# Two transposes moved from TensorE to VectorE: Wv and the rows of sequences 3 and 4 loaded in blocks, with the rows of Wq, Wk and Wp in matching order

## The chip, the cores and the metric

The kernel runs on one core of one Trainium2 chip. The time is device microseconds of one execution; it was run three times. One further execution was taken by the hardware profiler, and all views of the profile come from that one. Engines are called PE (TensorE matmul), PEld (TensorE weight load), DVE (VectorE), ACT (ScalarE), POOL (GpSimd) and SP (SyncE, which only issues DMAs here). A line such as L489 is a line of the kernel before.

## The reference

Four sequences of 512 tokens with 512 features, all in fp32. An attention block, two feed-forward blocks and a low-rank adapter follow each other:

```python
q = x @ Wq; k = x @ Wk; v = x @ Wv                    # x [4,512,512], W* [512,512]
attn = softmax(q @ k.T * 512**-0.5)
attn_out = (attn @ v) @ Wp + bp
cms = gelu(attn_out @ cW1 + cb1) @ cW2 + cb2 + one_hot(codes)   # hidden 2048
mod = gelu(concat([attn_out, cms]) @ mW1 + mb1) @ mW2 + mb2
x1 = clip(x + cms + mod, 0, 1)
h = x1 + gelu(x1 @ W_down[stream] + b_down[stream]) @ W_up[stream] + b_up[stream]
out = (h - mean) * rsqrt(var + 1e-5) * ln_w[stream] + ln_b[stream]
```

## The kernel before, in words

The sequences are handled in two pairs. Features lie on partitions (four chunks of 128), tokens along the free dimension. All matmuls are fp32. Products are made by a scheme that needs seven block products in place of eight (on two levels in the feed-forward blocks); the price is sums of blocks, which DVE and POOL make.

**The folded weights.** The scores are x (Wq Wk^T) x^T, so the kernel first makes Wq Wk^T, and likewise Wv Wp (`folded`, L744). For a product both operands need the contracted index on partitions, so Wq, Wk, Wv and the rows of x are transposed first. PE does all of that: `begin_transposed` (L484) issues 16 transposes of 128x128 into four PSUM banks (`tr_ps`, L489), whose `end` then empties them; `turned_quarter` (L863, transposes at L868) does it for quarters of Wq and Wk.

**Where the transposed tiles go.** `left_from_psum` (L720, for Wv), `right_from_psum` (L677) and `second_operand.take` (L560, both for x) copy each bank to SBUF on ACT (L725, L683, L571) and make the block sums on DVE (L547, L558), part of them straight from PSUM.

**One product.** `seven` (L591) runs the seven block products in the order that it is given, in numbers 1 to 7, for one or two rows of blocks. Product 1 is copied out as c1 by ACT (L612); when product 5 is there, DVE adds c1 to it ("c15"); when 6 is there, DVE adds c15 to it into the bank of 5 ("the y sum"); when 7 has been accumulated onto 6, DVE makes v from it and c15 ("the v sum"), into a bank of its own; only then may product 4 accumulate further onto that bank. 3 accumulates onto y, 2 onto 1. `pair_product` (L632, matmuls at L637) uses the order 1, 2, 5, 6, 7, 4, 3 on 512 columns for both sequences of a pair at once; `small_product` (L694, matmuls at L703) uses 256 columns. Work can be hung behind a number by `then`. The recording layer orders the instructions of each engine itself, by dependences and estimates, unless one is pinned by `keep_in_program_order`; so the order in the text is not quite the order on the engine. PSUM has eight banks, all from one pool.

**Order around the change.** SP loads Wq in quarters (ACT's queue Wk), then x of sequences 1 and 2 (`load_x`, L141), Wv and Wp (`weight`, L114), into big[0], big[1], slot[2], slot[3]. POOL's queue loads the first part of cW1 and x of 3 and 4 into slot[6], slot[7]. PE turns and multiplies Wq and Wk; x of 1 and 2 are turned in between (`first_operand`, `both_operands`, L839 and L845). The first `pair_product` (x times the folded matrix) has the transposes of Wv behind its product 7 (L932). Then Wv Wp, the scores and softmax of sequences 1 and 2 (L946, sums of the second's x by `left_sums` at L951), the products with the probabilities, and a second `pair_product` (L982), which has x of sequence 3 turned behind its product 6 and x of 4 behind its 4. The second pair follows in the same way without loads.

**POOL's background work.** `expansion` (L420) makes the block sums of cW1, cW2 and mW1 from 13 us to 339 us and stores them in DRAM through spaces that the pair's layers use later (`part`, `first`, `wide`); `steps` (L473) advances it. The layers load them by SP into `wslot`. From 207 us on SP's queue is in use; before that it is empty after the first loads. ACT's queue stores the turned x (`xT_kept`, L857), which POOL loads back and adds to cms much later (L1688, L1691).

Of the kernel before, what the change touches and what calls it, by code (L numbers as in the profile page):

```python
# [8 lines left out]
F32 = mybir.dt.float32  # L9
# [9 lines left out]
def kernel(  # L19
# [119 lines left out]
    make_identity(nc, ident)  # L139

    def load_x(b, eng, dst):  # L141
        eng.dma_start(out=dst, in_=x[b].rearrange("(t p) v -> p t v", p=P))
        return dst
# [51 lines left out]

    def weight_sums(a11, a12, a21, a22, s1, s2, s3, s4, eng=None):
        eng = eng or nc.gpsimd
        eng.tensor_tensor(s1, a21, a22, ALU.add)
        eng.tensor_tensor(s2, s1, a11, ALU.subtract)
        eng.tensor_tensor(s3, a11, a21, ALU.subtract)  # L200
        eng.tensor_tensor(s4, a12, s2, ALU.subtract)  # L201

# [6 lines left out]


    def flat(t):
        return t.rearrange("p c n -> p (c n)")

# [229 lines left out]
    def inner_weights(src, is_first, store, p, u):  # L443
# [27 lines left out]
        }  # L471

    def steps(gen, n):  # L473
        for _ in range(n):
            next(gen, None)

# [7 lines left out]
    def begin_transposed(get, dst, finish=None):  # L484

        ps = [bank("tr_ps") for d in range(4)]
        for c in range(4):
            for d in range(4):
                nc.tensor.transpose(  # L489
                    ps[d][:, c * P : (c + 1) * P], get(c)[:, d * P : (d + 1) * P], ident  # L490
                )

        def end():
            for d in range(4):
                if finish is None:
                    evacuate(dst[:, d, :], ps[d])
                else:
                    finish(d, ps[d])

        return end  # L500

    def chunks(t):
        return lambda c: t[:, c, :]

# [162 lines left out]

    def left_sums(t, s):
        weight_sums(*halves(t), *(s[:, k] for k in range(4)))

# [98 lines left out]

    xT_kept = [spill.tile([P, 4, 512], F32, name=f"xT_kept{b}") for b in range(B)]  # L770
    attn_kept = [spill.tile([P, 4, 512], F32, name=f"attn_kept{b}") for b in range(B)]
# [63 lines left out]
    def places(pair):  # L835

        return big[2 + 2 * pair : 4 + 2 * pair], (big[6:8], big[0:2])[pair]

    def first_operand(pair):  # L839
        xT, t_x = places(pair)  # L840
        return begin_transposed(
            chunks(x_rows[2 * pair]), xT[0], right_from_psum(xT[0], sums_in(flat(t_x[0])))
        )

    def both_operands(pair):  # L845
        xT, _ = places(pair)
        operands, take = second_operand(*xT, mod)
        beside = right_from_psum(xT[1], sums_in(flat(places(pair)[1][1])), copy=False)
        transposed(
            chunks(x_rows[2 * pair + 1]), xT[1],  # L850
            lambda d, ps: take(
                d // 2, (slice(d % 2, d % 2 + 1), slice(0, 512)),
                ps.rearrange("p (c n) -> p c n", c=1), lambda: beside(d, ps),
            ),
        )
# [56 lines left out]
    for pair in range(B // 2):  # L912
# [14 lines left out]
        if pair == 0:  # L927
# [14 lines left out]
        def turn(k):  # L942
            transposed(lambda t: mod[k][:, t, :], pT[k], right_from_psum(pT[k], t_p[k]))

        for k in range(2):
# [711 lines left out]
    for pair in range(B // 2):  # L1657
# [144 lines left out]
```

## Time and profile before

| | us |
|---|---|
| three runs | 1171.57, 1169.13, 1168.83 |
| median | 1169.13 |
| profiled execution, its own time | 1169.93 |
| profiled execution, span from the first to the last instruction | 1168.2 |
| PE busy | 1158.7 (99%) |
| DVE busy | 893.8 (77%) |
| POOL busy | 588.6 (50%) |
| ACT busy | 293.2 (25%) |

In the table of busy times a matmul's record includes its way through the array, and records overlap. So a group's own cost on PE is read from the start of one group to the start of the next in the chain of waits, not from the mean length of a record. A record of an fp32 matmul appears twice (two passes), that of a transpose once. For DVE and ACT too, the step from one instruction to the next in a run without idle time is shorter than a record: 0.60 us against 0.69 for 128x512 on DVE.

The phases by start time: folding of Wq and Wk to 25 us, first pair's attention to 129, its projection with the turning of x of 3 and 4 to 143, second pair's attention to 243, the first pair's feed-forward blocks to 676, the second pair's to the end, with the first pair's adapters inside.

### The profile page before, as it was taken

How to read it: one execution, taken by the hardware profiler on the slowest of the kernel's cores; microseconds unless marked ns; L12 is line 12 of the kernel's file. 1: busy time of each engine (PE TensorE's matmuls, PEld its weight loads, DVE VectorE, ACT ScalarE, POOL GpSimd, SP SyncE). 2: the span in 40 equal slices, each digit the busy share in tenths (PEclk: the TensorE clock that was granted, in tenths of full speed). 3: DMA queues.
4: the chain of work that ended last, by engine and by line, in shares of the span. 5: the costliest groups of instructions: out<-in, count | busy, mean ns of one | idle time of the engine just before them, and what ended most of it. 6: DMA issues, size and time to landing. Idle time of an engine off the chain costs nothing.

```text
span 1168.2 us, 13723 instructions
## 1 busy us (share of the span) xinstructions
PE 1158.7 (99%) x4989; PEld 927.4 (79%) x4989; DVE 893.8 (77%) x1215; ACT 293.2 (25%) x535; POOL 588.6 (50%) x652
## 2 busy tenths in 40 slices
PE   9999999999999999999999999999999999999997
PEld 8588558657468888888888887778888888888875
DVE  5755655587699967899699956689994588689956
ACT  4244315236520000012310027271000003220014
POOL 4989999988897058982200636972000001242101
PEclk9999999999999999999999999999999999999999
DMA  9742784897766588896847662135745454594701
GB/s 336 268 139 100 297 323 176 307 382 253 300 240 245 185 282 313 322 328 263 258 157 279 191 215 90 64 143 179 299 132 188 168 216 180 176 307 165 246 6 73
DMA packets 81283, 256.80 MB, mean 220 GB/s; under 512 B 7956, under 2 KB 38976, under 8 KB 65984
## 3 DMA queue, kind: packets, MB, share of 16 engines
q1 hardware_dynamic: 56864, 152.98, 36.4%
q0 software_dynamic: 21968, 93.37, 22.7%
q10 hardware_dynamic: 2384, 9.57, 2.1%
q8 instruction: 40, 0.66, 0.2%
q14 instruction: 27, 0.22, 0.1%
HBM read 186.69 MB, written 66.06 MB: 216 GB/s over the span
## 4 chain that ended last, share of the span: by engine, by line
PE 94%; DVE 2%; POOL 1%; DMA 1%; issue 1%; DVEq 0%
PE i L1406 29%; PE i L1306 26%; PE sum L1148 9%; PE sum L703 9%; PE sum L637 8%; PE c L1238 6%; PE down_ps L1512 2%; PE up_ps L1531 2%; PE tr_ps L489 1%; DMA wslot<-in_L_cond_mW 1%; PE up_ps L1526 1%; DVE slot L206 1%; DVE hidden L547 1%; PE tr_ps L868 0%; PE idle_ps L193 0%
## 5 line engine op out<-in xcount | busy, mean ns | idle before, releaser
L1306 PE MATMUL i<-slot,wslot 128*128 128x256 f32 x1184 | 261.4, 379 | 1.3 <-DVE part L1010 1.2
L1306 PEld LDWEIGHTS i<-slot,wslot 128*128 128x128 f32 x1184 | 224.7, 190 | 32.8 <-issue 1.8
L1406 PE MATMUL i<-slot,wslot 128*128 128x256 f32 x896 | 202.5, 379 | 0.0
L1406 PEld LDWEIGHTS i<-slot,wslot 128*128 128x128 f32 x896 | 170.2, 190 | 23.1
L1017 ACT COPY first<-i 128x256 f32<-128x256 f32 (+1 forms) x56 | 26.7, 477 | 516.0 <-PE i L1406 255.6
L1406 PE MATMUL i<-hidden,wslot 128*128 128x256 f32 x576 | 132.2, 379 | 0.0
L1406 PEld LDWEIGHTS i<-hidden,wslot 128*128 128x128 f32 x576 | 109.4, 190 | 15.7 <-issue 1.0
L1010 DVE TENSOR_TENSOR part<-i,part 128x512 f32<-128x512 f32 (+1 forms) x156 | 90.5, 591 | 37.7 <-PE i L1306 25.4
L1039 ACT ACTIVATE hidden<-hidden,bias 128x512 f32<-128x512 f32 x128 | 83.9, 716 | 81.3 <-DVE hidden L547 71.3
L1688 POOL DMA_DIRECT2D slot<-xT_kept x4 | 2.7, 683 | 152.9 <-PE i L1306 152.9
L1148 PE MATMUL sum<-mod,wslot 128*128 128x256 f32 x288 | 66.7, 379 | 0.2 <-DVE sum L547 0.2
L206 DVE TENSOR_TENSOR slot<-hidden 128x1024 f32<-128x1024 f32 x46 | 61.3, 1332 | 0.0
L1148 PEld LDWEIGHTS sum<-mod,wslot 128*128 128x128 f32 x288 | 54.6, 190 | 7.9 <-DVE sum L547 0.6
L1691 POOL TENSOR_TENSOR cms<-cms,slot 128x512 f32<-128x512 f32 x16 | 24.4, 1548 | 71.3 <-PE i L1306 41.1
L1010 DVE TENSOR_TENSOR part<-i,first 128x512 f32<-128x512 f32 (+1 forms) x62 | 36.3, 589 | 29.0 <-PE i L1306 17.7
L547 DVE TENSOR_TENSOR sum<-sum,wslot 128x512 f32<-128x512 f32 x48 | 33.3, 696 | 31.5 <-PE sum L703 19.6
L206 DVE TENSOR_TENSOR slot<-hidden,slot 128x1024 f32<-128x1024 f32 x46 | 56.8, 1234 | 0.3
L1238 PE MATMUL c<-slot,wslot 128*128 128x512 f32 x128 | 55.3, 592 | 0.0
L547 DVE TENSOR_TENSOR hidden<-part,hidden 128x2048 f32<-128x2048 f32 x20 | 54.6, 2732 | 0.5
L703 PE MATMUL sum<-hidden,wslot 128*128 128x256 f32 x232 | 53.4, 380 | 0.6 <-POOL wslot L201 0.6
L703 PEld LDWEIGHTS sum<-hidden,wslot 128*128 128x128 f32 x232 | 43.7, 190 | 6.7 <-POOL wslot L201 1.0
L1238 PEld LDWEIGHTS c<-slot,wslot 128*128 128x128 f32 x128 | 24.3, 190 | 30.6 <-issue 27.5
(338 smaller groups left out, 2129.3 us busy)
## 6 DMA issues: line engine op xcount, KB each, us to landing
wslot<-m_kept SPq DMA_DIRECT2D x48, 1024.0 KB
wslot<-m_kept SPq DMA_DIRECT2D x36, 512.0 KB
wslot<-c_kept SPq DMA_DIRECT2D x16, 1024.0 KB
slot<-in_L_cond_mW POOLq DMA_DIRECT2D x24, 512.0 KB
wslot<-in_L_cond_mW SPq DMA_DIRECT2D x24, 512.0 KB
wslot<-in_L_cond_cW SPq DMA_DIRECT2D x40, 256.0 KB
slot<-in_L_cond_cW POOLq DMA_DIRECT2D x16, 512.0 KB
m_kept<-wide POOLq DMA_DIRECT2D x6, 1024.0 KB
```

Of the source, the lines that this page charges most:

```text
L206: i = eng.tensor_tensor(out_, one, two, ALU.subtract)
L547: nc.vector.tensor_tensor(dst, a, b, ALU.add)
L637: nc.tensor.matmul(ps, lhsT=lhs[p][:, c, r * P : (r + 1) * P], rhs=rhs[p][:, c, :], start=(first_ and c == 0), stop=(c == 1), skip_group_c ...
L703: nc.tensor.matmul(v[:, j, :], lhsT=lhs[p][:, c, j * P : (j + 1) * P], rhs=rhs[p][:, c, :], start=(first_ and j == 0 and c == 0), stop=(c ...
L1010: nc.vector.tensor_tensor(dst, ps, other, ALU.add)
L1017: nc.scalar.copy(c1, p1)
L1039: nc.scalar.activation(block[:, t, :], block[:, t, :], AF.Gelu, bias=bias_c[:, 8 * half + t : 8 * half + t + 1],)
L1148: nc.tensor.matmul(halves_of(ps)[:, j, :], lhsT=a[g][:, at_[q], j * P : (j + 1) * P], rhs=rhs[q][:, 0, :], start=(first_ and j == 0), stop ...
L1238: nc.tensor.matmul(ps, lhsT=lhs(c, t), rhs=operands[p][:, c, :], start=(c == 0), stop=(c == 1),)
L1306: nc.tensor.matmul(out_ps[:, j, :], lhsT=a[j][q][:, c, :], rhs=now[q][:, c, :], start=(c == 0), stop=(c == 1),)
L1406: nc.tensor.matmul(ps[:, :256], lhsT=a[k // 2][q][:, k % 2, :], rhs=now[q][:, k, :], start=(k == 0), stop=(k == 3),)
L1691: nc.gpsimd.tensor_tensor(cms[s][:, d, :], cms[s][:, d, :], in_rows[3][:, d, :], ALU.add)
```

## The change

Wv, and x of sequences 3 and 4, are loaded by four DMAs each, one for each group of 32 partitions: partition 32a + r receives, for each of the 16 groups t of 32 rows, the 128 consecutive elements (512 bytes) of row 32t + r that begin at column 128a. VectorE's transpose works on blocks of 32x32; four of its instructions, each of 128x512 with a step of four elements (16 bytes) on the input, turn the whole matrix into four PSUM banks, so that partition p of bank d holds column 4p + d. The 48 transposes of PE for these three matrices go.

The feature that partition p of chunk d stands for is thus 4p + d instead of 128d + p. Everything that is contracted with it follows: Wq, Wk and Wp are loaded with rows 4p + c (Wp by one DMA), and PE's transposes of x of sequences 1 and 2 read every fourth element. The turned x is stored to DRAM by features, and read back by 128c + p.

x of sequences 3 and 4 is needed untransposed as well, so SP loads it a second time into the same places once DVE has read them. The first load of these two moves in POOL's queue behind the first third of the expansion. The turning of Wv hangs behind product 6 of the first `pair_product` instead of 7. The sums of the x of sequence 2 are pinned, and the expansion's next steps are issued behind them.

```diff
@@ quarters (Wq, Wk)
-            rows, columns = slice(256 * r, 256 * r + 256), slice(256 * k, 256 * k + 256)
+            chunks, columns = slice(2 * r, 2 * r + 2), slice(256 * k, 256 * k + 256)
             eng.dma_start(
-                out=w[:, 2 * r : 2 * r + 2, columns],
-                in_=src[rows, columns].rearrange("(c p) n -> p c n", p=P),
+                out=w[:, chunks, columns],
+                in_=src.rearrange("(p c) n -> p c n", c=4)[:, chunks, columns],
             )
@@ loads
+    def load_blocks(src, dst, eng):
+        for a in range(4):
+            eng.dma_start(
+                out=dst[32 * a : 32 * a + 32].rearrange("p (t n) -> p t n", n=P),
+                in_=src[:, P * a : P * a + P].rearrange("(t r) n -> r t n", r=32),
+            )
+        return dst.rearrange("p (t c d) -> p d t c", d=4, c=32)
+
     x_rows = [load_x(b, nc.sync, x_places[b]) for b in range(2)]
-    wv = weight((nc.sync, nc.sync), Wv, slot[2])
-    wp = weight((nc.sync, nc.sync), Wp, slot[3])
+    x_blocks = []
+    wv = load_blocks(Wv, slot[2], nc.sync)
+    wp = slot[3].rearrange("p (c n) -> p c n", c=4)
+    nc.sync.dma_start(out=wp, in_=Wp.rearrange("(p c) n -> p c n", c=4))
@@ weight_sums
+        i = op(s1, a21, a22, ALU.add)
+        if pinned:
+            tc.keep_in_program_order(i)
...
@@ expansion
         load_c1(0)
+        yield from expand_c1(0, lambda: load_c1(1))
         for b in range(2, B):
-            x_rows.append(load_x(b, nc.gpsimd, x_places[b]))
-        yield from expand_c1(0, lambda: load_c1(1))
+            x_blocks.append(load_blocks(x[b], flat(x_places[b]), nc.gpsimd))
         yield from expand_c1(1, lambda: load_raw(cW2, False, 0, slot[4:6]))
@@ steps
+    behind = []
     def steps(gen, n):
-        for _ in range(n):
-            next(gen, None)
+        with tc.issue_after(behind.pop().ins) if behind else nullcontext():
+            for _ in range(n):
+                next(gen, None)
@@ transposes
+    def begin_turned(blocks, dst, finish=None):
+        ps = [bank("tr_ps") for d in range(4)]
+        for d in range(4):
+            nc.vector.transpose(ps[d].rearrange("p (t c) -> p t c", c=32), blocks[:, d])
+        def end():
+            for d in range(4):
+                if finish is None:
+                    evacuate(dst[:, d, :], ps[d])
+                else:
+                    finish(d, ps[d])
+        return end
+
+    def begin_x(b, dst, finish):
+        if b > 1:
+            return begin_turned(x_blocks[b - 2], dst, finish)
+        return begin_transposed(
+            lambda c: x_rows[b][:, c, :].rearrange("p (n d) -> p d n", d=4), dst, finish
+        )
@@ both_operands
         for k in range(2):
-            nc.scalar.dma_start(out=xT_kept[2 * pair + k], in_=xT[k])
+            nc.scalar.dma_start(
+                out=xT_kept[2 * pair + k].rearrange("(p c) n -> p c n", c=4), in_=xT[k]
+            )
+            if pair:
+                x_rows.append(load_x(2 + k, nc.sync, x_places[2 + k]))
@@ pairs
-            then[7] = [lambda: transposed(chunks(wv), wv_t, left_from_psum(wv_t, s_v))]
+            then[6] = [lambda: begin_turned(wv, wv_t, left_from_psum(wv_t, s_v))()]
...
-                left_sums(x_rows[s1], s_x[1])
+                behind.append(left_sums(x_rows[s1], s_x[1], pinned=True))
@@ with_input
-            tc.keep_in_program_order(nc.gpsimd.dma_start(out=in_rows[3], in_=xT_kept[2 * pair + s]))
+            tc.keep_in_program_order(nc.gpsimd.dma_start(out=in_rows[3], in_=xT_kept[2 * pair + s].rearrange("(c p) n -> p c n", p=P)))
```

More of the change, by code (lines that the diff above doesn't have):

```diff
@@ L1 @@
-from contextlib import ExitStack
+from contextlib import ExitStack, nullcontext
 import concourse.bass as bass
@@ L139, with flat @@
     make_identity(nc, ident)
+    def flat(t):
+        return t.rearrange("p c n -> p (c n)")
     def load_x(b, eng, dst):
@@ L193, with weight_sums @@
         nc.tensor.matmul(idle_ps[:, :P], lhsT=zeros, rhs=zeros, start=True, stop=True)
[L196 to L201, printed above, removed]
+    def weight_sums(a11, a12, a21, a22, s1, s2, s3, s4, eng=None, pinned=False):
+        op = (eng or nc.gpsimd).tensor_tensor
+        i = op(s1, a21, a22, ALU.add)
+        if pinned:
+            tc.keep_in_program_order(i)
+        op(s2, s1, a11, ALU.subtract)
+        op(s3, a11, a21, ALU.subtract)
+        return op(s4, a12, s2, ALU.subtract)
     def token_sums(b11, b12, b21, b22, t1, t2, t3, t4, eng=None, pinned=False):
@@ L208, in token_sums @@
                 tc.keep_in_program_order(i)
-    def flat(t):
-        return t.rearrange("p c n -> p (c n)")
     C1_PLAIN = {1: (0, 0), 2: (1, 0), 4: (1, 1)}
@@ L489, in begin_transposed @@
                 nc.tensor.transpose(
-                    ps[d][:, c * P : (c + 1) * P], get(c)[:, d * P : (d + 1) * P], ident
+                    ps[d][:, c * P : (c + 1) * P], get(c)[:, d], ident
                 )
@@ L500, in begin_transposed @@
         return end
+    def begin_turned(blocks, dst, finish=None):
[9 more added lines that the diff above has]
+        return end
     def chunks(t):
-        return lambda c: t[:, c, :]
+        return lambda c: t[:, c, :].rearrange("p (d n) -> p d n", n=P)
     def into(t):
@@ L666, in left_operand, with left_sums @@
         return {1: a11, 2: a12, 3: s4, 4: a22, 5: s1, 6: s2, 7: s3}
-    def left_sums(t, s):
-        weight_sums(*halves(t), *(s[:, k] for k in range(4)))
+    def left_sums(t, s, pinned=False):
+        return weight_sums(*halves(t), *(s[:, k] for k in range(4)), pinned=pinned)
     def right_operand(t, s):
@@ L768, in folded @@
         return left_operand(w, s)
-    xT_kept = [spill.tile([P, 4, 512], F32, name=f"xT_kept{b}") for b in range(B)]
+    xT_kept = [spill.tile([V, T], F32, name=f"xT_kept{b}") for b in range(B)]
     attn_kept = [spill.tile([P, 4, 512], F32, name=f"attn_kept{b}") for b in range(B)]
@@ L837, in places @@
         return big[2 + 2 * pair : 4 + 2 * pair], (big[6:8], big[0:2])[pair]
+    def begin_x(b, dst, finish):
[4 more added lines that the diff above has]
+        )
     def first_operand(pair):
         xT, t_x = places(pair)
-        return begin_transposed(
-            chunks(x_rows[2 * pair]), xT[0], right_from_psum(xT[0], sums_in(flat(t_x[0])))
+        return begin_x(
+            2 * pair, xT[0], right_from_psum(xT[0], sums_in(flat(t_x[0])))
         )
@@ L848, in both_operands @@
         beside = right_from_psum(xT[1], sums_in(flat(places(pair)[1][1])), copy=False)
-        transposed(
-            chunks(x_rows[2 * pair + 1]), xT[1],
+        begin_x(
+            2 * pair + 1, xT[1],
             lambda d, ps: take(
@@ L854, in both_operands @@
             ),
-        )
+        )()
         for k in range(2):
-            nc.scalar.dma_start(out=xT_kept[2 * pair + k], in_=xT[k])
+            nc.scalar.dma_start(
[3 more added lines that the diff above has]
+                x_rows.append(load_x(2 + k, nc.sync, x_places[2 + k]))
         return operands
@@ L942, in turn @@
         def turn(k):
-            transposed(lambda t: mod[k][:, t, :], pT[k], right_from_psum(pT[k], t_p[k]))
+            transposed(chunks(mod[k]), pT[k], right_from_psum(pT[k], t_p[k]))
         for k in range(2):
```

## The prediction

> **What bounds the kernel now.** I read the page's busy table first, then who waited for whom on PE, then the chain of waits in order of time, then the stages in which the removed work lies.
>
> ```profile
> PE 1158.7 (99%) x4989; PEld 927.4 (79%) x4989; DVE 893.8 (77%) x1215; ACT 293.2 (25%) x535; POOL 588.6 (50%) x652
> ```
>
> PE is busy for 1158.7 of 1168.2 us, so a microsecond taken from PE's queue is a microsecond of the span, unless a new wait replaces it. PE's waits before 220 us are two:
>
> ```profile
> PE idle_ps L193 <- DVE zeros L190: 1.1, 1, 1.1
> PE sum L703 <- POOL wslot L201: 0.6, 1, 0.6
> ```
>
> The chain, in order of time (start, length), passes through the transposes that the change takes away:
>
> ```profile
> 43.08 0.87 PE tr_ps L489 x8
> 43.95 1.72 PE sum L637 x4
> 45.67 0.44 PE tr_ps L489 x4
> ...
> 48.68 0.44 PE tr_ps L489 x4
> ...
> 111.89 3.72 PE sum L703 x16
> ...
> 129.35 1.75 PE tr_ps L489 x16
> ...
> 138.93 1.64 PE tr_ps L489 x15
> ```
>
> Wv is turned at 43 to 49 us, x of sequence 3 at 129 to 131, of sequence 4 at 135 to 141. Sixteen take 1.75 us, so one takes 0.109 us of PE however long its own record is (272 ns; records overlap). The two stages (length, then busy time and instructions of each engine):
>
> ```profile
> 25.00:51.00 26.00, 26.00 (x75) 12.43 (x74) 20.17 (x44) 9.23 (x18) 21.86 (x24) 1.00 0.76 277
> 129.00:150.00 21.00, 21.00 (x74) 11.15 (x73) 15.27 (x32) 9.10 (x16) 20.94 (x23) 1.00 0.71 285
> ```
>
> Third of the busy times is DVE: 20.2 of 26 and 15.3 of 21 us. DVE has room there, but not much, and it is DVE that gets the work.
>
> **The change part by part.** The sum is against the profiled execution: span 1168.2 us, time 1169.93, so 1.7 us lie around the span; it is 0.8 us above the median of the runs, 1169.13.
>
> *Removed from PE.* 48 of the 144 transposes of L489 (the group on slot tiles): 48 x 0.109 = 5.24 us, all on the chain. *Removed wait.* At 111.89 PE waited 0.58 us for POOL's sums of x of sequence 2 (L198 to L201 into wslot). In the new order these four stand right behind the second part of the cW1 expansion and ahead of the cW2 expansion. Adding POOL's rows up from 53.4 us (eight x loads, the five sums and six DMAs between) they end near 86, against a need at 109: 0.58 us gained.
>
> *Added on DVE.* Twelve block transposes of 128x512 elements, SBUF to PSUM, reading every fourth element (16 bytes apart). No such instruction and no such step is in the trace. The nearest rows:
>
> ```profile
> L547 DVE TENSOR_TENSOR sum<-sum,wslot 128x512 f32<-128x512 f32 x10 | 7.0, 697 | 7.8 <-PE sum L703 5.0 <-PE sum L637 2.9
> L198 POOL TENSOR_TENSOR wide<-slot 128x512 f32<-128x512 f32 x2 | 2.5, 1272 | 0.0
> 330.45 3.94 DVE L206 TENSOR_TENSOR slot<-hidden 128x1024 f32<-128x1024 f32 x1
> 344.62 1.23 DVE L206 TENSOR_TENSOR slot<-hidden,slot 128x1024 f32<-128x1024 f32 x1
> ```
>
> DVE's 128x512 operations record 0.69 us and follow each other every 0.60; ACT copies that size every 0.48, a floor; POOL works through it every 1.23 us; and one DVE operation from SBUF took 3.94 us beside busy POOL where its like takes 1.23, a factor of 3.2. So T, the step from one block transpose to the next, lies between 0.48 and about 1.9 us. I take 0.60, the row of the same engine, size and PSUM side, and walk both places in the built order.
>
> First place (before's clock). DVE ends the y sum of row 1 near 39.4 us, then does four transposes, eight 128x256 sums of Wv (0.33 each, 2.66), then the two v sums (0.60 each) that order 7 of the product leaves. PE ends order 7 at 42.06 and now does order 3 first (3.44 us) and one matmul of the next product (0.43), to 45.93; order 4 needs the first v sum, ready at 39.4 + 4T + 2.66 + 0.6 = 42.7 + 4T. At T = 0.60 that is 45.1: no stall; from T = 0.81 on PE waits; 1.6 us at 1.2; 4 at 1.8.
>
> Second place (clock from the product's start, 115.45). DVE: second c15 sum to 11.2, T, y, T, y, 2T, eight sums, v. The second y waits for PE until 13.9, so v is ready at 17.8 + 2T, or at 15.7 + 4T if that is later. PE needs it at 19.75. T = 0.60: 19.0, no stall. At 1.2: 0.8 us, and 0.4 more behind the second four, whose results the next product's orders 5 and 6 need. At 1.8 about 6 us, since both fours then hold up PE.
>
> So the wait costs 0 at 0.60, 2.9 at 1.2, about 10 at 1.8; a faster T than 0.60 gains nothing.
>
> [...]
>
> *Strided loads on PE.* The 32 transposes of sequences 1 and 2 stay, but load weights with a 16-byte step:
>
> ```profile
> L489 PEld LDWEIGHTS tr_ps<-ident,hidden x32: 139/140/143, 15.7 to 24.7; 128*128 128x128 f32 x32
> ```
>
> A load of 140 ns hides behind a step of 109. If the step lengthened it, PE could be held to at most the 190 ns of other fp32 loads: 32 x 0.081 = 2.6 us. A gain has no reason: the stream of columns is as long. I take 0.5, keep 0 and 2.6.
>
> *Costed at nothing.* Quarters of Wq and Wk: same 1 KB runs, same bytes. Wv in 512-byte runs: needed at 39 us instead of 43; at the 329 GB/s of the first 25 us the 6 MB up to it and Wp take some 19, so its own 1 MB (3 us) could take four times as long. POOL issues eight x loads in place of two: 8 x 0.76 against 1.51, +4.6 us on POOL near 55 us; 2.1 us of gathers move behind the expansion, and the 7.5 us wait of L361 for the c_outer store shrinks, so POOL reaches the cW2 sums some 2 us earlier. Reloading x of 3 and 4 on SP: its queue is empty until 207, the sums that read them are at 157 and about 170, issues at 129 and 138; behind them on SP stands only the attention reload of 207. The load of xT_kept in 2 KB runs on POOL: 0.1 us an issue, its sums have PE to wait for. If the POOL cover fails: at 336 to 350 DVE reuses wide, whose last store landed near 334.5 by its DMA packets, and PE then lives on its eight banks; 5 us of late POOL would cost 3 to 5 us.
>
> Sum: 1169.93 - 5.24 - 0.58 + 0.5 = 1164.6; for the median, 1169.13 - 5.3 = **1163.8**.
>
> **The rivals.**
> *B: block transposes at half pace (T = 1.2, as POOL's row).* 1169.13 - 5.8 + 2.9 + 0.5 = 1166.7; at T = 1.0 it is 1165. For it: the 16-byte step. Against: no row shows DVE slower for a layout.
> *C, slower: DVE becomes the bound in both places, because block transposes from SBUF stretch beside POOL as the row of 3.94 us did.* Price 10 us at T = 1.8: 1169.13 - 5.8 + 10 + 0.5 = 1173.8; it decides from T of about 1.45 on. For it: POOL is busy 20.9 of 21 us in the second place. Against: DVE's operations with one SBUF and one PSUM operand keep 0.60 there.
> *D: strided weight loads set PE's pace*, +2.6: 1165.9 with T = 0.60, more with B.
> *E: the gain is given back at 336 to 350 us*, where PE arrives 5 us earlier and POOL does not: about 1168.8. Against: 334.5 leaves 1.7 us to the 336.2 at which DVE would want wide, and POOL is some us earlier.
> That the change does not do what it says is excluded: the built PE queue has 48 transposes fewer.
>
> **How the numbers follow.** Forecast 0.45, B 0.27, C 0.20, D 0.05, E 0.03. A difference under 0.3% (3.5 us) is about what a measurement of this kernel cannot tell from none. Faster by more: the forecast and half of B (T up to 1.05), 0.45 + 0.13 = 0.58. Within: the rest of B 0.14, D 0.04, E 0.02 = 0.20. Slower: C 0.20, and 0.01 each of D and E = 0.22. The range goes from 1162.0 (all 5.8 us, no strided price, less the 1.3 us that a run may lie lower) to 1172.0, which takes in B, D, E and C up to T = 1.65, and leaves out about 0.1 of C and 0.05 below.
>
> **What would show it.** In the profile after: 96 transposes by PE at this line, steps of 0.109 us also for hidden tiles (D if their sixteens take over 2 us); twelve DVE transposes with a step of 0.60 (B near 1.2, C over 1.45); PE without a wait for DVE near 46 and 133 us, and none for POOL near 109; PE reaching the first c matmul (L1238) near 237.6 instead of 242.9 and the first L1306 as much earlier. The forecast is wrong if PE waits over 1 us for a v sum at either place, or if the lead at 243 us is there but gone at 420.

## Result, and the profile after

The changed kernel takes 1172.49 us (median of 22 runs, 1167.29 to 1178.41), the kernel before 1169.39 (22 runs, 1167.69 to 1171.57): a ratio of 1.0034, 95% interval 1.0023 to 1.0046. Predicted were 1163.8 us. It is slower by a third of a per cent, little, but the whole interval lies above 1, and its runs spread over 11.1 us instead of 3.9. Its profiled execution took 1172.08 us, span 1170.3, against 1169.93 and 1168.2 before.

In the profile after, L489 has become L506, the block transposes are L523, L547 is L579, L637 is L669, L703 is L735, L868 is L911, L1010 and L1017 are L1053 and L1060, L1238 is L1281, L1306 is L1349, L1326 is L1369, L1406 is L1449.

The busy table of the page, as shown of before:

```profile
PE 1155.4 (99%) x4941; PEld 923.0 (79%) x4941; DVE 904.5 (77%) x1227; ACT 294.1 (25%) x535; POOL 605.2 (52%) x658
```

PE has 48 instructions fewer and is busy for 3.3 us less, DVE has 12 more; yet the span is 2.1 us longer. Who waited for whom on PE (sum, times, longest):

```profile
PE i L1449 <- DVE cms L1053: 2.5, 1, 2.5
PE i L1449 <- ACT first L1060: 1.7, 1, 1.7
PE i L1349 <- DVE part L1053: 1.5, 1, 1.5
PE idle_ps L208 <- DVE zeros L205: 1.1, 1, 1.1
PE sum L669 <- DVE sum L579: 0.9, 1, 0.9
PE i L1349 <- DMA wslot<-in_L_cond_mW: 0.4, 2, 0.2
PE tr_ps L911 <- DMA wide<-in_L_cond_Wk: 0.2, 1, 0.2
```

The wait for POOL's sums is gone. Five rows are new: the two of L1449, which had no wait before, that of L669, and two short ones for loads. The chain that ended last shows what PE waited for; first the page's shares by engine, then pieces of the chain (start, length):

```profile
PE 72%; POOL 16%; DMA 6%; DVE 3%; issue 2%; ACTq 0%; DVEq 0%; POOLq 0%
```

```profile
2.30 8.49 DMA wide<-in_L_cond_Wk
...
40.51 4.11 DVE tr_ps L523 x4
48.11 3.70 PE sum L669 x8
51.81 32.81 PE sum L735 x152
...
204.59 8.56 DMA m_kept<-part
...
249.61 10.54 DMA m_kept<-part
...
336.59 4.16 DMA m_kept<-wide
```

Before, the chain was PE's for 94% and POOL's for 1%. Now it leaves PE at 86 us and follows POOL's expansion and the landing of its stores until 341 us. The two stages of the prediction (length, busy time and instructions of PE, PEld, DVE, ACT, POOL, granted clock, DMA share, GB/s):

```profile
25.00:51.00 26.00, 25.12 (x67) 11.63 (x66) 24.24 (x49) 8.97 (x17) 20.07 (x22) 1.00 0.62 225
129.00:150.00 21.00, 20.97 (x50) 9.11 (x49) 20.93 (x39) 9.10 (x15) 20.94 (x23) 1.00 0.87 299
```

DVE rises from 20.2 to 24.2 us of 26 and from 15.3 to 20.9 of 21: it is nearly full in the first place and full in the second.

**Where the time goes.** The start of the same PE work after, less its start before, through the run:

| at (time before) | after less before, us |
|---|---|
| 15.9, x of sequence 1 turned | +0.70 |
| 24.9, first pair product | +1.07 |
| 83.9, first softmax's transposes | +0.53 |
| 113.7, behind the removed POOL wait | -0.30 |
| 167.0 to 335.7, second pair, first c layer | -3.51 |
| 420.3, first L1349 | **+1.25** |
| 876.8 | +0.97 |
| 1046.0, and to the end | +1.84 |

So the change does bring 3.5 us (5.3 were expected), keeps them until 336 us, and loses 4.8 us in one layer. PE's order there, with its waits, and the ACT copy that it waits for:

```profile
344.32 1.89 PE L1449 MATMUL i<-hidden,wslot 128*128 128x256 f32 x8
347.93 1.99 PE L1449 MATMUL i<-slot,wslot 128*128 128x256 f32 x8 [1.72 <-ACT first L1060]
352.42 3.72 PE L1449 MATMUL i<-slot,wslot 128*128 128x256 f32 x16 [2.49 <-DVE cms L1053]
```

```profile
347.50 0.65 ACT L1060 COPY first<-i 128x256 f32<-128x256 f32 x2 [7.19 <-DMA m_kept<-first]
```

The copy goes into the space `first`, which POOL's expansion still uses: its last store from there has to land. POOL issues it at 342.94 us; before, at 338.32:

```profile
342.94 0.56 POOL L392 DMA_DIRECT2D m_kept<-first  x1
```

```profile
338.32 0.56 POOL L378 DMA_DIRECT2D m_kept<-first  x1
```

So PE is 3.5 us earlier and POOL 4.6 us later. The larger of the two waits, 2.49 us, comes another way, through DVE. DVE writes into `wide`, another of the expansion's spaces; its last store was issued at 336.59 us, 6.6 us later than before (329.95). DVE waits for its landing, and then its operation takes 4.09 us where it took 2.27 before (after, then before):

```profile
341.07 4.09 DVE L1369 TENSOR_TENSOR wide<-hidden,hidden 128x2048 f32<-128x2048 f32 x1 [1.55 <-DMA m_kept<-wide]
```

```profile
341.17 2.27 DVE L1326 TENSOR_TENSOR wide<-hidden,hidden 128x2048 f32<-128x2048 f32 x1
```

At this place of the run the operation took, in the fifteen profiles of this case, 2.27 or 2.28 us where POOL had issued its last store of the expansion before it began, and 3.5 to 4.3 us where POOL was not done. So a late POOL costs in two ways here: by the landing of its stores, and, as these profiles suggest, by slowing DVE.

**Why POOL is late.** Its first operation of the expansion, after and then before:

```profile
30.69 1.27 POOL L213 TENSOR_TENSOR wide<-slot 128x512 f32<-128x512 f32 x1 [9.50 <-DMA slot<-in_L_cond_cW]
```

```profile
29.09 0.72 POOL L198 TENSOR_TENSOR wide<-slot 128x256 f32<-128x256 f32 x1 [6.66 <-PE sum L637]
```

Before, cW1 is there and POOL waits for PE; after, POOL waits for cW1. While cW1 should arrive, the DMA engines are full and move half as much (stage 15 to 20 us, after and before; the last two columns are DMA share and GB/s):

```profile
15.00:20.00 5.00, 5.00 (x33) 4.62 (x32) 2.66 (x6) 1.68 (x4) 4.98 (x6) 1.00 1.22 181
```

```profile
15.00:20.00 5.00, 5.00 (x33) 4.55 (x32) 3.18 (x8) 2.05 (x4) 4.98 (x6) 1.00 1.05 388
```

What is loaded there is Wv, by groups of 32 partitions: SP issued its four DMAs from 6.95 to 13.93 us. The experiments take this up. By then the theories were: (1) POOL's expansion, late, sets the end, and PE's lead is lost to it, at first put down to the place of the sums of sequence 4; (2) POOL is late because of the more and smaller DMAs and the second load of x; (3) VectorE's block transposes are what costs.

### The profile page after: what moved, and what is told of

Same layout as the page of the kernel before. It is cut to its first block, busy times and chain, and to the rows that moved or that the text cites. A ratio compares the mean times of both kernels' runs of the same rounds, so it can differ in the third digit from the quotient of the medians.

```text
span 1170.3 us, 13661 instructions
## 1 busy us (share of the span) xinstructions
PE 1155.4 (99%) x4941; PEld 923.0 (79%) x4941; DVE 904.5 (77%) x1227; ACT 294.1 (25%) x535; POOL 605.2 (52%) x658
## 4 chain that ended last, share of the span: by engine, by line
PE 72%; POOL 16%; DMA 6%; DVE 3%; issue 2%; ACTq 0%; DVEq 0%; POOLq 0%
PE i L1449 28%; PE i L1349 26%; PE sum L1191 7%; PE sum L735 4%; DMA m_kept<-part 3%; PE down_ps L1555 2%; PE up_ps L1574 2%; PE sum L669 1%; POOL part L213 1%; DMA wslot<-in_L_cond_mW 1%; DMA c_kept<-wide 1%; POOL part L216 1%; POOL slot L361 1%; POOL part L217 1%; POOL first L375 1%
## 5 line engine op out<-in xcount | busy, mean ns | idle before, releaser
L1349 PE MATMUL i<-slot,wslot 128*128 128x256 f32 x1184 | 261.7, 379 | 1.8 <-DVE part L1053 1.5
L1349 PEld LDWEIGHTS i<-slot,wslot 128*128 128x128 f32 x1184 | 224.6, 190 | 33.7 <-issue 2.4
L1449 PE MATMUL i<-slot,wslot 128*128 128x256 f32 x896 | 202.9, 379 | 4.2 <-DVE cms L1053 2.5
L1449 PEld LDWEIGHTS i<-slot,wslot 128*128 128x128 f32 x896 | 170.1, 190 | 28.1 <-DVE cms L1053 2.9
L1060 ACT COPY first<-i 128x256 f32<-128x256 f32 (+1 forms) x56 | 26.7, 479 | 519.3 <-PE i L1349 239.7
L1449 PE MATMUL i<-hidden,wslot 128*128 128x256 f32 x576 | 132.2, 379 | 0.0
L1449 PEld LDWEIGHTS i<-hidden,wslot 128*128 128x128 f32 x576 | 109.4, 190 | 15.7 <-issue 1.0
L1053 DVE TENSOR_TENSOR part<-i,part 128x512 f32<-128x512 f32 (+1 forms) x156 | 90.5, 591 | 35.2 <-PE i L1349 25.7
L1082 ACT ACTIVATE hidden<-hidden,bias 128x512 f32<-128x512 f32 x128 | 83.9, 716 | 82.8 <-DVE hidden L579 72.7
L1734 POOL TENSOR_TENSOR cms<-cms,slot 128x512 f32<-128x512 f32 x16 | 28.9, 1832 | 75.8 <-PE i L1349 51.2
L1053 DVE TENSOR_TENSOR part<-i,first 128x512 f32<-128x512 f32 (+1 forms) x62 | 36.3, 589 | 27.1 <-PE i L1349 17.5
L1281 PE MATMUL c<-slot,wslot 128*128 128x512 f32 x128 | 55.3, 592 | 0.0
L579 DVE TENSOR_TENSOR hidden<-part,hidden 128x2048 f32<-128x2048 f32 x20 | 54.0, 2698 | 0.5
L735 PE MATMUL sum<-hidden,wslot 128*128 128x256 f32 x232 | 53.2, 379 | 0.0
L579 DVE TENSOR_TENSOR sum<-sum,wslot 128x512 f32<-128x512 f32 x48 | 33.0, 693 | 23.2 <-PE sum L735 19.7
L1281 PEld LDWEIGHTS c<-slot,wslot 128*128 128x128 f32 x128 | 24.3, 190 | 30.6 <-issue 28.5
L735 PEld LDWEIGHTS sum<-hidden,wslot 128*128 128x128 f32 x232 | 43.8, 190 | 5.8
```

The lines of the kernel that those rows point to most:

```text
L579: nc.vector.tensor_tensor(dst, a, b, ALU.add)
L735: nc.tensor.matmul(v[:, j, :], lhsT=lhs[p][:, c, j * P : (j + 1) * P], rhs=rhs[p][:, c, :], start=(first_ and j == 0 and c == 0), stop=(c ...
L1053: nc.vector.tensor_tensor(dst, ps, other, ALU.add)
L1060: nc.scalar.copy(c1, p1)
L1082: nc.scalar.activation(block[:, t, :], block[:, t, :], AF.Gelu, bias=bias_c[:, 8 * half + t : 8 * half + t + 1],)
L1281: nc.tensor.matmul(ps, lhsT=lhs(c, t), rhs=operands[p][:, c, :], start=(c == 0), stop=(c == 1),)
```

## The experiments

**1. POOL's sums of sequence 4 later.** After the change, POOL makes these four sums at 173 us; before, at 201, where they fill a wait for a store.

```diff
             s_x[1] = sums_in(flat(attn[1]))
-            left_sums(x_rows[s1], s_x[1])
...
         steps(expanding, 6 if pair else 4)
+        if pair:
+            left_sums(x_rows[s1], s_x[1])
```

> The changed kernel, with one edit: POOL's four block sums of x of sequence 4 (5.0 us) are issued behind the six expansion steps of the second pair instead of ahead of them, which puts them back near 200 us, where they stood before. Theory 1 (POOL's expansion sets the end since the change): the sums fill the time in which POOL waits for the landing of its m_kept store, as before; the last store of the expansion (m_kept<-first) is issued near 338.5 us instead of 342.9, the two PE waits in the first L1449 layer (1.72 and 2.49 us) go, PE keeps its 3.5 us, and the time falls by 4.2 to 4.8, to 1167 to 1168. Theory 2 (POOL is late because of the more and smaller DMAs and the second load of x): the store stays within a microsecond of 342.9 and the time within a microsecond of the changed kernel, 1171 to 1173. Theory 3 (VectorE's transposes are what costs): no change, 1172.

Measured: 1170.08 us (1166.63 to 1177.72, 12 runs), ratio 1.0011, 0.9998 to 1.0024. Six of 12 runs are under 1170, two of 22 of the changed kernel. But in the profiled execution, the slowest of the twelve at 1177.72 us, cW1 landed still later, POOL began at 32.47, the last store was issued at 344.68 and not at 338.5, and PE waited 6.3 us. The sums are at most part of the cause; theory 1 was right about the place and not yet about the reason.

**2. PE's lead taken away.**

```diff
+    pad_ps = bank("pad_ps")
+    for _ in range(8):
+        tc.keep_in_program_order(nc.tensor.matmul(
+            pad_ps, lhsT=zeros, rhs=mod[0][:, 0, :], start=True, stop=True
+        ))
     load_attn(0, (6, 7))
```

> The changed kernel with eight more matmuls of 128x512 on PE, whose result nobody reads, just ahead of the first c matmul (L1281, 239 us): 8 x 0.43 = 3.4 us more work on PE, so that PE has no lead there. Theory 1 (POOL decides at 345 us whether PE comes early or not): PE's waits at 347 to 352 us shrink by the same 3.4 us, from 4.2 to about 0.8, and the time stays at 1172 to 1173. Rival (PE's own queue is the path): 3.4 us slower, 1175.5.

The eight matmuls are 16 records in the trace and take 6.9 us (239.33 to 246.19), 0.86 us for one, twice what was meant:

```profile
239.33 7.03 PE L1700 MATMUL pad_ps<-mod,zeros 128*128 128x512 f32 x16
```

Measured: 1173.11 us (5 runs, ratio 1.0040, 1.0027 to 1.0053), 0.6 us above the changed kernel. PE is 3.3 us late instead of 3.5 early at 336 us and waits 1.8 us instead of 4.2. Of the 6.9 us, 4.2 are left behind the layer (425.75 us against 421.59) and 2.5 in the span. 3.3 of the 6.9 us go beyond the lead and have to cost; so, as an estimate from these numbers, the lead of 3.5 us is worth about 1 us behind the layer. Theory 1 said next to nothing.

**3. Block transposes of neighbouring elements.**

```diff
-        return dst.rearrange("p (t c d) -> p d t c", d=4, c=32)
+        return dst.rearrange("p (t d c) -> p d t c", d=4, c=32)
```

> The changed kernel with the block transposes reading 32 elements that lie next to each other instead of every fourth (the features then stand in another order than the rows of Wq, Wk and Wp, so this part of the computation is changed). If the 16-byte step on the input makes the transpose slow, four take about 2.4 us instead of 4.1, and PE's wait of 0.88 us for the v sum at 48 us goes. If a block transpose of fp32 takes 1.03 us whatever the step, four still take 4.1 and the wait stays. By theory 1 the end moves by less than a microsecond either way, 1171 to 1173, because what PE gains early is lost at 345 us; by the rival that VectorE's transposes are what costs, a faster transpose gives 1169 or less.

This kernel leaves out that the rows of Wq, Wk and Wp have to follow the features, so what it computes is not the reference's result; only its times are of use.

The instructions of the tile in which the transposes land (count, minimum, median, maximum in ns), with the 16-byte step and without:

```profile
L523 DVE STREAM_TRANSPOSE tr_ps<-slot x12: 1078/1106/1117, 40.5 to 139.2; 128x512 f32<-128x512 f32 x12
```

```profile
L523 DVE STREAM_TRANSPOSE tr_ps<-slot x12: 682/696/717, 40.7 to 137.3; 128x512 f32<-128x512 f32 x12
```

Four take 4.11 us with the step and 2.49 without, so 1.03 and 0.6 us each. The wait for the v sum is gone, PE's lead at 243 us is 3.95 instead of 3.51 us. The time is not better: 1174.81 us (6 runs), ratio 1.0047, 1.0028 to 1.0065. cW1 was late again (POOL began at 31.80) and PE waited 7.6 us at L1449. So theory 3 does not explain the loss: transposes at 0.6 us bring PE 0.4 us and do not save the kernel.

**4. Wv and Wp as before, x of 3 and 4 by VectorE.**

```diff
-    wv = load_blocks(Wv, slot[2], nc.sync)
-    wp = slot[3].rearrange("p (c n) -> p c n", c=4)
-    nc.sync.dma_start(out=wp, in_=Wp.rearrange("(p c) n -> p c n", c=4))
+    wv = weight((nc.sync, nc.sync), Wv, slot[2])
+    wp = weight((nc.sync, nc.sync), Wp, slot[3])
...
-            then[6] = [lambda: begin_turned(wv, wv_t, left_from_psum(wv_t, s_v))()]
+            then[7] = [lambda: transposed(chunks(wv), wv_t, left_from_psum(wv_t, s_v))]
```

> The changed kernel with Wv and Wp as before: loaded in 2 KB runs, Wv turned by PE behind product 7 in 16 transposes; x of sequences 3 and 4 stay with VectorE. PE gets 16 x 0.109 = 1.75 us back, and loses the wait of 0.88 us. It also tells where the 1.07 us that PE is late at 25 us come from: if from Wv's 512-byte runs, which share the DMA engines with the first quarters, they go, and POOL's first expansion operation starts near 29 instead of 30.7 us; if from the order of the rows of Wq and Wk, both stay. PE's lead at 239 us is then about 3.7 us in the first case and 2.6 in the second. By theory 1 the end follows POOL: 1170 to 1171 if POOL starts 1.6 us earlier, 1172 if not. By the rival (the transposes of Wv on VectorE are what costs) it falls below 1169.

Measured: 1168.13 us, ratio 1.0001, 0.9989 to 1.0012. The stage 15 to 20 us moves 388 GB/s again, POOL begins at 25.7 us. PE is still 1.36 us late at 25 us: so there are two things at the start, Wv's load, which delays POOL, and the order of the rows, which delays PE. The last store is at 341.17, and PE waits 1.8 us; the next experiment puts that down to the sums of sequence 4. By its time alone this run fits theory 3 too, which expected less than 1169 without DVE's transposes of Wv. Experiment 6, which keeps them all, rules that out.

**5. Both edits (1 and 4).**

> The two edits of the runs before together: Wv and Wp loaded and Wv turned as before the change (POOL's first store then stands at 34.4 us, as before the change, instead of 37 to 41), and the block sums of x of sequence 4 behind the six expansion steps. Theory 1, now with two causes (Wv's 512-byte runs hold up the first load of cW1 and with it POOL's start; the sums of sequence 4 moved ahead leave POOL waiting for its own stores later): the last store of the expansion is issued at 338.5 us or earlier, against 341.2 with Wv by PE alone and 344.7 with the sums alone; PE's waits at 345 us go and its lead of 2.65 us stays: 1166 to 1167. If the sums don't matter, the store stays near 341 and the time near 1168.

Measured: 1167.36 us, ratio 0.9986, 0.9978 to 0.9995; last store at 336.02, no wait at L1449. PE lost 1.9 us to a DVE sum at 257 to 280 us instead, and had them back at 591.

**6. Wv behind cW1.** The change stays whole; only the queue of Wv's four loads is another.

```diff
-    wv = load_blocks(Wv, slot[2], nc.sync)
...
         load_c1(0)
+        x_blocks.append(load_blocks(Wv, slot[2], nc.gpsimd))
...
```

> The changed kernel with Wv's four loads on POOL's queue behind the first loads of cW1, instead of on SP's queue ahead of them; nothing else. Theory 1: cW1 lands near 27 us again, POOL's first store is issued near 34.4 instead of 37 to 41 us, and all of POOL is 3 to 6 us earlier than in the runs of the changed kernel; the last store is issued near 340 us, PE's waits at 345 us shrink to 0 to 1.5 us, the runs scatter less, and the time is 1167 to 1168.5. VectorE's transposes of Wv start no later than now (the y sum holds them to 40 us), unless Wv lands after 40: then PE's wait at 48 us grows from 0.9 by as much. If 512-byte runs on the DMA engines are not what delays POOL, 1172 stays.

Measured: 1166.47 us, ratio **0.9983**, 0.9971 to 0.9994: 6 us less than the changed kernel, from where four DMAs stand. POOL's first operation waits for PE again, the last store is issued at 336.96, and of PE's waits in L1449 this is left:

```profile
29.39 0.73 POOL L212 TENSOR_TENSOR wide<-slot 128x256 f32<-128x256 f32 x1 [5.03 <-PE sum L669]
```

```profile
PE sum L669 <- DVE sum L579: 0.9, 1, 0.9
PE i L1449 <- DVE cms L1053: 0.3, 1, 0.3
```

It still is not the kernel of the forecast: the wait for the v sum is there, and PE waits 1.3 us for quarters of Wq and Wk and is 2.2 us late at 25 us.

**7. The same with the sums of sequence 4 later.**

> Both causes taken away with the change's transposes kept: Wv's loads behind cW1 on POOL's queue, and the sums of sequence 4 behind the six expansion steps. Theory 1: the last store is issued at 338.5 us or earlier, PE does not wait at 345 us, and its lead of 3.5 us at 239 us is still there at 421: 1169.1 - 3.5 = 1165.6. If the lead is lost in another place, 1167 to 1169.

Measured: 1166.74 us, ratio 0.9982, 0.9972 to 0.9992. The place of the sums makes no difference here. In experiments 4 and 5, where POOL's first store is in time as well (34.35 and 34.22 us), it moved the last store by 5.2 us; why it does so there and not here was not taken apart.

**8. The order of the rows alone**, in the kernel before.

```diff
@@ quarters
-                in_=src[rows, columns].rearrange("(c p) n -> p c n", p=P),
+                in_=src.rearrange("(p c) n -> p c n", c=4)[:, chunks, columns],
@@ transposes of x
-            chunks(x_rows[2 * pair]), xT[0], ...
+            by_four(x_rows[2 * pair]), xT[0], ...
...
```

> The kernel before with the order of the rows alone: Wq and Wk loaded by rows 4p + c, PE's transposes of all four x reading every fourth element, the turned x stored and read back by features; Wv, x of 3 and 4 and all loads else as before, all turned by PE. If the row order is what makes PE 1.1 to 1.4 us late at 25 us in all changed kernels so far, it shows here too, and 64 strided weight loads add 4 x 0.2 us: 1.9 to 2.2 us later at 239 us, 1171. If Wv's runs delay the first quarters, PE is on time at 25 us and the kernel within 1 us of before.

Measured: 1170.93 us, ratio 1.0012, 1.0003 to 1.0021. PE is 1.34 us late at 16 us, after waiting 0.9 us for quarters of Wq and 0.7 for Wk, and 1.74 at 25 us; sixteen strided transposes take about 0.2 us more than others.

**9. Quarters merged.** Version 6, with the two later quarters of Wq and of Wk as one DMA each.

```diff
-        for r, k in QUARTERS:
-            chunks, columns = slice(2 * r, 2 * r + 2), slice(256 * k, 256 * k + 256)
+        for r, columns in ((0, slice(0, 256)), (0, slice(256, 512)), (1, slice(0, 512))):
+            chunks = slice(2 * r, 2 * r + 2)
```

> The kernel with Wv's loads behind cW1, and the two later quarters of Wq, and of Wk, loaded by one DMA each: with rows 4p + c these are 4 KB runs instead of pieces of 1 KB. If short pieces are why the row order makes PE wait for Wq and Wk at 7 to 12 us (1.2 to 2.2 us late at 25 us in all kernels with that order, 1.74 with the row order alone), PE is at most 1 us late at 25 us and the kernel gains about 1 us on the version with Wv behind cW1 (1166.5): 1165.5. If it is the distance of the rows that a quarter touches, or a later landing of the larger pieces costs as much, it stays at 1166.5 or gets up to 1 us slower.

Measured: PE does not wait for Wq or Wk and is 0.97 us late at 25 us, as expected. Ratio 0.9983, 0.9974 to 0.9992 (1166.05 us beside 1167.97 for before on that chip): no gain over version 6 that can be told from nothing. The last store is at 328.03, and the lead of 3.35 us passes L1449 whole.

**10 and 11. POOL delayed, nothing else**: in version 6, and in the kernel before.

```diff
         nc.gpsimd.dma_start(out=c1_inner[1, u], in_=slot[1][:, 1024:])
+        if u == 0:
+            for _ in range(2):
+                nc.gpsimd.tensor_tensor(flat(first), slot[4][:, :1024], slot[5][:, :1024], ALU.add)
```

> The kernel with Wv's loads behind cW1 (1166.5, 0.9983 of before), with two more POOL additions of 128x1024 (2 x 2.35 = 4.7 us), whose result nobody reads, in the first third of the expansion at 32 us. It puts back POOL's late start, and nothing else, no slow load and no other order of the DMAs. If POOL's late start is what costs in the changed kernel: the first store is issued near 39 us, the last (m_kept<-first) at 341 to 344 instead of 337, PE waits 2 to 6 us in the first L1449 layer, and the time is 1169 to 1174, with scatter. If POOL's later waits absorb the 4.7 us (they sum to 14.9 us), the last store stays near 337 to 338 and the time at 1166.5 to 1167.5; then Wv's load on SP's queue costs in another way.

> The kernel before the change with the same two POOL additions at 32 us. It shows how much POOL's lateness costs where PE has no lead. If the price is set by how late POOL is against PE: PE reaches the first L1406 layer 2.4 us later than the kernel with Wv's loads behind cW1, so it waits some 2 us less than that one with the same delay: 0 to 3 us slower than before, 1169 to 1172. If PE's lead has nothing to do with it, both lose the same.

Measured: version 6 goes from 0.9983 to **1.0059**, 1.0043 to 1.0074 (1175.96 us, more than was expected), the last store to 343.63. PE's waits in this layer, whose line is L1452 here, are the very pair that the changed kernel has:

```profile
PE i L1452 <- DVE cms L1056: 2.5, 1, 2.5
PE i L1452 <- ACT first L1063: 1.7, 1, 1.7
```

The kernel before goes to 1.0025, 1.0014 to 1.0035; there PE waits 1.6 and 0.6 us for POOL's sums of sequence 2 near 112 us, so it comes 2.6 us later to L1406 and waits 1.4 us there. So a late POOL alone is enough for the changed kernel's picture at the layer, at a price that was larger where PE had a lead: 0.76% against 0.25%.

**12 and 13. What makes Wv's load slow**: 512-byte runs, or 32 partitions?

```diff
@@ 12: changed kernel, all partitions, same runs
-    wv = load_blocks(Wv, slot[2], nc.sync)
+    for t in range(16):
+        nc.sync.dma_start(
+            out=slot[2][:, P * t : P * t + P],
+            in_=Wv[32 * t : 32 * t + 32].rearrange("r (a n) -> a r n", n=P),
+        )
...
@@ 13: kernel before, groups of 32, 2 KB runs
-    wv = weight((nc.sync, nc.sync), Wv, slot[2])
...
+    for a in range(4):
+        nc.sync.dma_start(
+            out=wv[32 * a : 32 * a + 32],
+            in_=Wv.rearrange("(c p) n -> p c n", p=P)[32 * a : 32 * a + 32],
+        )
```

> The changed kernel with Wv loaded at the same place of SP's queue, in the same 512-byte runs to the same addresses, but by 16 DMAs that reach all 128 partitions each (one for each group of 32 rows) instead of 4 that reach 32 partitions each. If the group of 32 partitions is what halves the rate of the load (181 GB/s from 15 to 20 us with the engines full, 388 before), the rate is above 330 GB/s again, cW1 lands before 29 us, POOL's first expansion operation no longer waits for it, the last store is issued near 337, and the time is 1166 to 1168. If the length of the runs is the cause, the rate stays near 180 and the time at 1172.

> The kernel before with Wv loaded by 4 DMAs of 32 partitions each, in 2 KB runs as before (same addresses, same transposes on PE). If the group of 32 partitions is the cause, the rate from 15 to 20 us falls from 388 to about 180 GB/s and POOL's first expansion operation waits for cW1 and starts 1 to 3 us later; the time rises by 0 to 3 us, as in the kernel before with POOL delayed (1171.2). If the 512-byte runs are the cause, the rate stays at 380 and nothing changes: 1169.

The first does not answer the question: SP took 24.9 us to issue 16 DMAs where it took 7.0 for the four, and PE waited 6.6 us at 26 us for the bias (1174.60 us, ratio 1.0048, 1.0033 to 1.0064); the stage moved 114 GB/s at a DMA share of 0.38, so the engines were not full and nothing follows. The second is clear. In 2 KB runs, 32 partitions at a time:

```profile
15.00:20.00 5.00, 5.00 (x33) 4.56 (x32) 3.19 (x7) 2.06 (x4) 4.99 (x6) 1.00 1.07 209
```

388 GB/s become 209 at full engines; POOL begins at 31.54, PE waits 1.2 and 0.9 us for its sums near 112 us (0.6 before), and the kernel *before* gets slower: 1173.93 us (7 runs), ratio 1.0046, 1.0030 to 1.0061. Its profile shows 2.6 us more span than before's; the rest of the 5.4 us that the ratio stands for does not show there. So loading by groups of 32 partitions is enough to halve the rate, with runs as long as before; what the short runs add (181 in the changed kernel against 209 here) was not taken apart, and why 32 partitions at a time move less is not shown by these runs.

**All runs in one table.** When POOL issues the last store from `first`, when PE begins the first L1449 layer (L1406 before), and what PE waits in it, all from the one profiled execution of each kernel:

| kernel | last store | PE at layer | store less PE | PE waits, us |
|---|---|---|---|---|
| version 9 | 328.0 | 332.4 | -4.4 | 0 |
| 5 | 336.0 | 335.1 | 0.9 | 0 |
| 8, rows alone | 339.4 | 337.3 | 2.0 | 0 |
| 13, before, groups of 32 | 339.9 | 337.9 | 2.1 | 0 |
| 12, Wv by 16 DMAs | 343.9 | 341.4 | 2.4 | 0 |
| before | 338.3 | 335.7 | 2.6 | 0 |
| 7 | 336.5 | 333.9 | 2.6 | 0 |
| 6 | 337.0 | 333.4 | 3.6 | 0.3 |
| 2, padded | 344.2 | 339.0 | 5.2 | 1.8 |
| 11, before, POOL delayed | 346.0 | 338.4 | 7.6 | 1.4 |
| 4 | 341.2 | 333.1 | 8.1 | 1.8 |
| **changed kernel** | 342.9 | 332.2 | 10.7 | 4.2 |
| 10, version 6, POOL delayed | 343.6 | 332.9 | 10.7 | 4.2 |
| 1 | 344.7 | 333.4 | 11.3 | 6.3 |
| 3 | 344.0 | 331.8 | 12.2 | 7.6 |

Up to some 3 us the store is in time. Beyond that PE pays, though not in strict order (1.8 us at 5.2, 1.4 at 7.6), since the waits come by two ways, through ACT and through DVE. Before had about a microsecond of room.

**What lies between the late start and the late store.** The first store's delay is not simply carried along. Beside version 6 POOL in the changed kernel's profile is 2.75 us late at its first store, 0.7 at 129 us and 1.6 at 204.6; then 4.9 at 214, 10.6 at 250 and 6.0 at the last store. It opens where POOL waits 3.29 us for a store to land at 213 us, and where three of its additions take 1.7 us each at 242 to 247. In experiment 10 POOL is 4.1 us behind version 6 at 129 us already, in 1, 2 and 3 2.9 to 4.7. That the place of Wv's load decides is shown by experiment 6, and that a late POOL is enough, by 10; how 1.6 us at 204.6 become 6 was not taken apart.

## Why the prediction was wrong

The direction was wrong. The three terms that stand in the sum held, or nearly; what was left out of it as free did not.

- *48 transposes, 5.24 us*: right. Over the second place PE gains 3.2 us of the 3.5 that 32 transposes cost; over the first it gains 0.5 of 1.75, most of the rest being the wait of 0.88 us below.
- *POOL's wait at 112 us*: right, it is gone (PE gains 0.83 us from 84 to 114 us).
- *Strided loads, 0.5 us*: right. Weight loads of hidden tiles take 209 ns for 140, and the two sixteens 0.16 and 0.21 us more.
- *T = 0.60*: wrong, 1.03; rival B was near. The walk gave a first v sum at 42.7 + 4T = 46.8 us against a need at 45.93, 0.9 us; PE waited 0.88. For the second place the walk gives 0.1 us at T = 1.03, and a few tenths behind it; 0.28 were lost. At T = 0.60 (experiment 3) the wait is gone, as the walk said. The row "same engine, same size" knew nothing of the step; rival B named it, with no row of before that showed its cost, and I gave it no price of its own. Experiment 3 has it: 1.03 us with the step of 16 bytes, 0.6 without.
- *"Costed at nothing", rows of Wq and Wk*: wrong, 0.7 us at 16 us, ahead of any strided transpose (1.34 in experiment 8). "Same runs, same bytes" does not say that the quarters arrive at the same time.
- *"Costed at nothing", Wv*: this is the step that failed first. I asked whether Wv itself would be there at 39 us, and it was. I did not ask who stands in the DMA engines behind it: cW1, for which POOL waits. The 5 us at half the rate became 3 to 7 us of delay of POOL's first store (34.3 us before, 37 to 41 in changed kernels with that load).
- *POOL reaches the sums of cW2 some 2 us earlier*: about right as far as it goes, 1.7 us at 129. *The argument against rival E*, that POOL is therefore earlier at 336 us too and `wide` free at 334.5: wrong, and the second step that failed. The sums of sequence 4 now went in at 173 us (5.0 us), SP's loads for PE, which was early, began at 203.5 instead of 207.0, and POOL waited 14.0 us in all for stores from `part` to land, 10.8 before. It was 5.0 us behind before at 231 us and 4.6 at the end; the store from `wide` landed at 340.75.

Rival E, at 0.03 and 1168.8 us, was the right mechanism at the right place. It was priced as PE's gain given back; POOL being later than before, which I excluded, makes it more than that. The prediction's own sign (a lead at 243 us that is gone at 420) is what the profile shows.

Forecast and measurement lie 8.7 us apart. Moving Wv's load gives back 6.0 of them. In version 6's profile the v sum's wait of 0.9 us, 1.3 us of waits for Wq and Wk, and 0.8 us between 877 and 1046 us are left, which is about the rest.

These last 0.8 to 0.9 us, lost between 877 and 1046 us, have an open cause: all kernels with block transposes lose them there (0.35 of it as PE's waits for wslot in the profile after), those without (experiments 8, 11 and 13) 0.2 or less.

## What to carry to other kernels

When an edit changes how something is loaded, look at what its load does to the loads beside and behind it, and follow those to the engine that waits for them; the load's own deadline is the smaller question. Before crediting a bound engine with a gain, write down every engine that runs along with it, and how many microseconds each has in hand where they meet: here PE could gain about 1 us before POOL had to be faster too. A new layout is not finished until its loads have their place in the queues: four DMAs in another queue turned 1.0034 into 0.9983.

## What the runs showed of the hardware

PE's waits in the first L1449 layer cost twice in experiments 1 and 3. Behind them, 6.3 us in all in experiment 1 and 7.6 us in experiment 3, the granted clock (the third column from the end) was not 1.00; experiment 1:

```profile
350.00:355.00 5.00, 1.29 (x3) 1.11 (x4) 4.97 (x7) 0.65 (x2) 4.09 (x4) 0.68 0.97 394
355.00:360.00 5.00, 5.00 (x16) 4.04 (x16) 4.86 (x8) 0.00 (x0) 3.78 (x5) 0.64 0.02 1
```

24 records of 128x256 took 7.7 us there, from start to start of the next group, and 5.2 elsewhere; in experiment 3 the clock was 0.95, 0.50 and 0.52 in the three stages from 345 to 360 us and they took 8.3. Behind the pair of 1.7 and 2.5 us it stayed at 1.00 in the changed kernel's profile and fell to 0.86 and 0.80, from 350 to 360 us, in that of experiment 10. If it stood at either 0.50 or 1.00 all the time, these stages hold an estimated 6.8 us at 0.50 in experiment 1, 10.3 in experiment 3 and 3.4 in experiment 10. The scatter goes with it: of the changed kernel's 22 runs the eleven above 1172.7 us have a mean granted clock of 0.994 to 0.996, the others 0.997 to 0.999. That 0.3% is an estimated 3.5 us of 1170, and the two halves' medians lie 4.5 apart; which waits those runs had is not on record. What makes the clock fall, and why the same pair of waits did it in one profile and not in the other, these runs do not show.

Where DVE and POOL worked side by side, one or both took longer in these places. POOL's additions of 128x256 took 1.7 us each at 242 to 247 us and 2.5 and 2.8 us at 323 to 328, beside DVE's work, and 0.72 for the most part; DVE's operation of 128x2048 took 4.09 us beside them at 341 us, and 2.27 where POOL had finished.
